# Graph attention on one core: seven block products inside one of the seven products of each 512x512 matrix product

## The chip, the cores and the metric

The kernel runs on one core of one Trainium2 chip. The metric is the device time of one execution in microseconds, and the number compared is the median over several executions. A second number, the span, comes from the profiler: the time from the first to the last instruction of one profiled execution.

The engines are named as in the profile: PE is the matrix engine (its weight loads are listed apart, as PEld), DVE the vector engine, ACT the scalar engine, POOL the general-purpose engine, and SP only starts transfers here.

## The reference

Two layers of graph attention on 128 graphs of 128 nodes with 512 features, all in fp32. `adj` is 128 matrices of 128x128.

```python
# layer 0 (8 heads of 64)
Q, K, V = x @ W_q + b_q, x @ W_k + b_k, x @ W_v + b_v
scores = einsum('bihd,bjhd->bhij', Q, K) / 8
scores = scores + (a[:, :, None] + c[:, None, :] + b_g + log(adj + 1e-9))   # a, c = x @ halves of w_g
x = einsum('bhij,bjhd->bihd', softmax(scores), V) + x
# layer 1
q, k, v = x @ Wq.T + bq, x @ Wk.T + bk, x @ Wv.T + bv
logits = einsum('bhqd,bhkd->bhqk', q, k) / 8 + log(clip(adj, 1e-8, None))
out = einsum('bhqk,bhkd->bhqd', softmax(logits), v) @ Wo.T + bo
return layer_norm(x + out) * gamma + beta
```

Of these only the seven 512x512 weight products per graph (three in layer 0, four in layer 1) are touched by the change.

## The kernel before

The graphs are worked on in groups of four, so there are 32 groups in each layer, and `t` counts the 64 of them. For every group each weight matrix is applied to 512 columns (four graphs of 128 nodes). This 512x512x512 product is cut in 2x2 blocks of 256 and done by Strassen's method in Winograd's form: seven products of 256x256x256 in place of eight, with sums of blocks ahead and behind. The sums of weight blocks are made once; the sums T1 to T4 of input blocks are made by POOL for each group.

```python
ORDER = ("P1", "P4 before", "P3 before", "P2", "P6", "P5", "P7")
OPERANDS = {
    "P1": (A11, "B11"), "P2": (A12, "B21"), "P3": (S4, "B22"), "P4": (NA22, "T4"),
    "P5": (S1, "T1"), "P6": (S2, "T2"), "P7": (S3, "T3"),
}
SUMS = {"T1": ("B12", "B11"), "T2": ("B22", "T1"), "T3": ("B22", "B12"), "T4": ("T2", "B21")}
```

`ORDER` is the order of a matrix's seven slots; "before" means the product belongs to the matrix before this one, so that two matrices overlap. One product is eight matmuls: two halves of the output, two of the depth, and each split in two column halves of 64 that write different halves of the partitions.

```python
def product(i, W, Bs, bank, side, first):
    a, b = Strassen.OPERANDS[i]
    a, b = W[:, a], Bs[b]
    for o in range(2):
        for k in range(2):
            ...                                  # dst: 256 columns of the bank, lhsT: 128x128, rhs: 128x256
            for half in HALVES:
                nc.tensor.matmul(dst[half], lhsT[:, half], rhs, start=(first and o == 0 and k == 0), stop=(k == 1),
                                 skip_group_check=True)
```

P1, P6, P7 and P4 add up in one bank of PSUM and are copied out by ACT between (t1, u2, u3); P5 and P3 share a second bank, P2 has a third. DVE adds.

```python
def unit(i):                                     # inside matrix()
    if i == "P1":
        t["W"], t["B"] = W(), Bs()
        t["a"] = bank(f"p{n % 2}")
    elif i == "P2":
        t["c"] = bank(f"p{(n + 1) % 2}")
    elif i == "P5":
        t["b"] = bank("p2")
    p = t[{"P2": "c", "P5": "b", "P3": "b"}.get(i, "a")]
    product(i, t["W"], t["B"], p, side, i in ("P1", "P2", "P5"))
    if i == "P1":   t["t1"] = kept("t1", p, 0)               # ACT copy, with the bias for q and k
    elif i == "P2": out_tile(); add(dst(0, 0), p, t["t1"])   # DVE
    elif i == "P6": t["u2"] = kept("u2", p, 0)
    elif i == "P7":
        t["u3"] = kept("u3", p, 1, 1)
        add(dst(1, 1), t["b"], t["u3"])                      # DVE
    elif i == "P4": copy(dst(1, 0), p, 1)                    # ACT
    elif i == "P3": add(dst(0, 1), p, t["u2"])               # DVE
```

Between the slots of the products lie a group's other steps, each put at a slot by number. `put(pre, i, ...)` sets a step ahead of slot i, `put(post, i, ...)` behind it; there are seven slots to a matrix, and every engine takes its instructions in this program order. In layer 0 the gate of each graph needs two sums of 512 products on DVE ("junk" in the profile), and POOL adds the bias row to the residual ("xn<-xn,bv", add_row).

```python
def gate(t, b, s):
    ...
    nc.vector.scalar_tensor_tensor(junk, XN[t, b // 2][:, b % 2], 1.0, WG[s], op0=ALU.mult, op1=ALU.mult,
                                   accum_out=C[t][:, s, b : b + 1])

def add_row(t, k):
    nc.gpsimd.tensor_tensor(XN[t, k], XN[t, k], wide(ROWS[split(t)[0]]), ALU.add)

def sums(Bs, name, tag, s):                      # T1 to T4, one buffer each
    a, b = Strassen.SUMS[s]
    Bs[s] = act.tile([P, 2, 2, N], F32, tag=f"{tag}{s}", name=f"{s}_{name}")
    nc.gpsimd.tensor_tensor(Bs[s], Bs[a], Bs[b], ALU.subtract)
...
if L == 0:
    for k, i in enumerate((6, 8, 9, 12, 14, 16, 18, 20)):
        put(post, first + i, gate, t, k // 2, k % 2)
    put(post, first + 20, gate_exp, t)
    for k in range(2):
        put(post, first + 21 + 2 * k, add_row, t, k)
```

`first` is the slot of v's P1 in group t. In layer 0 a group has the matrices v, q, k (slots 0 to 20); in layer 1 v, q, k and then o of the group before (28 slots). The scores of a group are made while the next two matrices run; its mixing with v follows three slots later.

Of the kernel before, what the change touches and what calls it, by code (L numbers as in the profile page):

```python
# [41 lines left out]
class Strassen:  # L42
# [6 lines left out]

    A11, A12, S4, NA22, S1, S2, S3 = range(7)  # L50

    ORDER = ("P1", "P4 before", "P3 before", "P2", "P6", "P5", "P7")
# [4 lines left out]
    SUMS = {"T1": ("B12", "B11"), "T2": ("B22", "T1"), "T3": ("B22", "B12"), "T4": ("T2", "B21")}  # L57

# [10 lines left out]
    @staticmethod  # L69
    def combine(v, t):  # L70
        v.tensor_tensor(t[:, Strassen.S1], t[:, Strassen.S3], t[:, Strassen.NA22], ALU.add)
        v.tensor_tensor(t[:, Strassen.S2], t[:, Strassen.S1], t[:, Strassen.A11], ALU.subtract)
        v.tensor_tensor(t[:, Strassen.S3], t[:, Strassen.A11], t[:, Strassen.S3], ALU.subtract)
        v.tensor_tensor(t[:, Strassen.S4], t[:, Strassen.A12], t[:, Strassen.S2], ALU.subtract)
        v.tensor_scalar_mul(t[:, Strassen.NA22], t[:, Strassen.NA22], -1.0)
# [26 lines left out]
def fast_path(ctx, tc, args, GOOD):  # L102
# [40 lines left out]
    def load_tiles(t):  # L143
        XT[t] = act.tile([P, G, KC, N], F32, tag="xT", name=f"xT_{t}", bufs=2)
        AD[t] = act.tile([P, G, N], F32, tag="adjT", name=f"adjT_{t}", bufs=3)
# [17 lines left out]
    def load(t):  # L163
        load_tiles(t)
        for b in range(G):
            load_graph(t, b, nc.sync)
        load_adjacency(t, nc.sync)
# [25 lines left out]
    def sums(Bs, name, tag, s):  # L193
        a, b = Strassen.SUMS[s]
        Bs[s] = act.tile([P, 2, 2, N], F32, tag=f"{tag}{s}", name=f"{s}_{name}")
        nc.gpsimd.tensor_tensor(Bs[s], Bs[a], Bs[b], ALU.subtract)


    def gate(t, b, s):

        if (b, s) == (0, 0):
            C[t] = small.tile([P, 2, G], F32, tag="c", name=f"c_{t}", bufs=3)
        junk = act.tile([P, D], F32, tag="oT3", name=f"junk_{t}_{b}_{s}")
        nc.vector.scalar_tensor_tensor(
            junk, XN[t, b // 2][:, b % 2], 1.0, WG[s], op0=ALU.mult, op1=ALU.mult,
            accum_out=C[t][:, s, b : b + 1],
        )
# [13 lines left out]

    def product(i, W, Bs, bank, side, first):
# [3 lines left out]
        a, b = W[:, a], Bs[b]  # L226
        for o in range(2):
            for k in range(2):
# [5 lines left out]
                for half in HALVES:  # L234
                    nc.tensor.matmul(
                        dst[half], lhsT[:, half], rhs, start=(first and o == 0 and k == 0), stop=(k == 1),
                        skip_group_check=True,
                    )

    def matrix(n, name, W, Bs, side, out_tile, dst, bias=None):  # L240


        t = {}

        def bank(tag):
            return ps.tile([P, 2, D2], F32, tag=tag, name=f"{tag}{name}")

        def shaped(v, o):
            return v.rearrange("p o (h d) -> p o h d", d=HD) if len(o.shape) == 4 else v

        def copy(o, i, m):

            if bias is None:
                nc.scalar.copy(o, shaped(i, o))
            else:
                for k in range(2):
                    c = 2 * m + k
                    nc.scalar.activation(o[:, k], i[:, k], AF.Identity, bias=bias()[:, c : c + 1])

        def kept(tag, i, m, bufs=2):  # L260
            o = work.tile([P, 2, D2], F32, tag=tag, name=f"{tag}{name}", bufs=bufs)
            copy(o, i, m)
            return o

        def add(o, i, v):
            nc.vector.tensor_tensor(o, shaped(i, o), shaped(v, o), ALU.add)

        def unit(i):
            if i == "P1":
                t["W"], t["B"] = W(), Bs()  # L270
                t["a"] = bank(f"p{n % 2}")
            elif i == "P2":
                t["c"] = bank(f"p{(n + 1) % 2}")
            elif i == "P5":
                t["b"] = bank("p2")
            p = t[{"P2": "c", "P5": "b", "P3": "b"}.get(i, "a")]
            product(i, t["W"], t["B"], p, side, i in ("P1", "P2", "P5"))
            if i == "P1":
                t["t1"] = kept("t1", p, 0)
            elif i == "P2":  # L280
                out_tile()
                add(dst(0, 0), p, t["t1"])
            elif i == "P6":
                t["u2"] = kept("u2", p, 0)
            elif i == "P7":
                t["u3"] = kept("u3", p, 1, 1)
                add(dst(1, 1), t["b"], t["u3"])
            elif i == "P4":
                copy(dst(1, 0), p, 1)
            elif i == "P3":  # L290
                add(dst(0, 1), p, t["u2"])

        return {i: (lambda i=i: unit(i)) for i in Strassen.OPERANDS}

    def v_matrix(n, t):
        L, _ = split(t)

        def tile_():
            V[t] = act.tile([P, G, H, HD + 1], F32, tag="v", name=f"v_{t}", bufs=2)
            nc.gpsimd.memset(V[t][:, :, :, HD : HD + 1], 1.0)  # L300
# [3 lines left out]
            lambda m, n: V[t][:, 2 * n : 2 * n + 2, 4 * m : 4 * m + 4, 0:HD],  # L304
        )

    def qk_matrix(n, t, which):
# [3 lines left out]
        def tile_():  # L311
            T[t] = act.tile([P, KC, G * N], F32, tag=f"{which}T", name=f"{which}T_{t}")
# [3 lines left out]
            lambda m, n: T[t][:, 2 * m : 2 * m + 2, n * D2 : (n + 1) * D2], lambda: bias[L],  # L316
        )

    def o_matrix(n, t):
        def tile_():  # L320
# [3 lines left out]
        return matrix(  # L324
            n, f"o_{t}", lambda: WO[1], lambda: TO[t], "x", tile_,
            lambda m, n: HS[t, n][:, :, m * D2 : (m + 1) * D2],
        )


    E = {}  # L330

    def scores(t, k):
# [4 lines left out]
        for b in (2 * k, 2 * k + 1):  # L337
            s[b] = ps.tile([P, 2, KC, N], F32, tag="s", name=f"s_{t}_{b}", bufs=2)
            rows = slice(b * N, (b + 1) * N)
            for c in range(KC):  # L340
                for r in range(2):
                    half = slice(r * HD, (r + 1) * HD)
                    nc.tensor.matmul(s[b][:, r, c], KT[t][half, c, rows], QT[t][half, c, rows], start=True, stop=True)
# [6 lines left out]
        for b in s:  # L350
            e = E[t, b]
            nc.vector.tensor_tensor(e, e, AD[t][:, b : b + 1].to_broadcast([P, H, N]), ALU.mult)

    def mix(t, graphs):
# [3 lines left out]
        for b in graphs:  # L358
# [3 lines left out]
            for h in range(H):  # L362
                for half in HALVES:
                    i = (h % KC) * (HD + 1)
                    nc.tensor.matmul(
                        a[b][half, h // KC, i : i + HD + 1], E[t, b][:, (h % 2) * KC + h // 2, half], V[t][:, b, h],
# [54 lines left out]
    def stats(t, b):  # L421
        if b == 0:
# [26 lines left out]
    def output_bias():  # L449

        p = ps.tile([P, 2, D2], F32, tag="p2", name="pbo")
        for m in range(2):
            for c in range(KC):
                nc.tensor.matmul(
                    p[:, m], bvcols[:, c], WO[1][:, Strassen.RAW[c // 2, m], c % 2],
# [6 lines left out]
    def strassen_weights(to, key, w, name, engine):  # L462
        to[key] = weights.tile([P, 7, 2, D2], F32, tag="w", name=name)
        Strassen.load(engine, to[key], w)
# [10 lines left out]
    def transposed(dst, src, name, copy, tag="t"):  # L475

        p = ps.tile([P, KC, N], F32, tag=tag, name=f"tr_{name}")
# [4 lines left out]
    for b in range(G):  # L482
        transposed(XT[0][:, b], XN[0, b // 2][:, b % 2], f"x_{b}", nc.vector.tensor_copy if b % 2 else nc.scalar.copy, ("t", "p2")[b % 2])
    TS[0] = quarters(XT[0])
    Strassen.combine(nc.vector, WV[0])
    for s in Strassen.SUMS:
        sums(TS[0], "0", "x", s)
    WG = [act.tile([P, D], F32, tag=f"oT{s + 1}", name=f"wg_{s}") for s in range(2)]
    for s in range(2):
        nc.sync.dma_start(WG[s], w_g[s * D : (s + 1) * D].partition_broadcast(P))  # L490
# [3 lines left out]
    ROWS[0] = row(nc, const, b_v0, "bv0")  # L494
# [3 lines left out]
    bvcols = act.tile([P, KC, P], F32, tag="oT4", name="bvcols")  # L498
    GA, BE = row(nc, const, gamma, "gamma"), row(nc, const, beta, "beta")
    ROWS[1] = row(nc, const, b_o1, "bo")  # L500
# [13 lines left out]
    for n in range(len(mats) + 1):  # L514
        for i in Strassen.ORDER:
            j, i = (n - 1, i[:2]) if "before" in i else (n, i)
            row_.append(mats[j][i] if 0 <= j < len(mats) else None)

    def slot(which, t, i):
        n = at[which, t] + ("before" in "".join(o for o in Strassen.ORDER if o.startswith(i)))  # L520
        return 7 * n + [o[:2] for o in Strassen.ORDER].index(i)

# [4 lines left out]

    for t in range(LAST):
        L, g = split(t)
        first = slot("v", t, "P1")  # L530

        a = slot("k", t, "P3") + 2
        put(pre, a, scores, t, 0)
        put(pre, a + 5, scores, t, 1)
        if t + 1 < LAST:
            put(pre, a + 3, mix, t, (0, 1))
            put(pre, a + 8, mix, t, (2, 3))
            put(post, a + 4, normalise, t, 0)
            put(post, a + 9, normalise, t, 1)
            put(post, a + 9, count, t)  # L540
        else:
            for b, i in enumerate((3, 4, 7, 8)):
                put(pre, a + i, mix, t, (b,))

        if t:
            put(post, first if L == 0 else first + 12, load_natural, t)
        if t + 1 < LAST:
            n = t + 1

            start = -1 if t == 0 else first + 7 if t > NG + 1 else first + 2  # L550
            put(post, start, load, n)
            start = max(start, 2)
            for b in range(G):
                put(post, start + 11 + b, lambda n, b: turn(XT[n][:, b]), n, b)
            put(post, start + 15, turn_adjacency, n)
            put(post, start + 15, lambda n: TS.update({n: quarters(XT[n])}), n)
            after = first + 20 if t <= NG else first + 25
# [336 lines left out]
```

## Time and profile before

| | |
|---|---|
| median of 3 executions | 3263.74 us (3263.38 to 3266.36) |
| span of the profiled execution | 3263.1 us |
| granted PE clock, mean | 0.998 |
| POOL, busy tenths in layer 0 and layer 1 | 2 to 3, and 5 |
| DVE, busy tenths in layer 0 and layer 1 | 5, and 4 |

The profile has a busy time for every engine, which says how full it is and not whether it is waited for. What sets the time is read from the chain of work that ended last (followed back from the last instruction) and from the list of waits, which names for each engine whom it waited for, with the total, the count and the longest. In the timeline a row is a run of equal instructions on one engine: its start, how long it lasted, what it writes and reads, and in brackets how long the engine had stood idle before and what ended that. The durations of rows of one engine overlap a little, since an instruction begins while the one before it drains.

The whole kernel is unrolled, and after the first group each layer repeats itself group by group. A group of layer 0 lasted 44.3 us (the T sums begin at 1017.76 and at 1062.03), one of layer 1 some 57 us.

### The profile page before, as it was taken

To read this page: it belongs to the slowest core of one execution; us is meant where nothing else is said; L and a number is where in the kernel's file an instruction comes from. 1 tells how busy PE (TensorE), PEld (TensorE's weight loads), DVE (VectorE), ACT (ScalarE), POOL (GpSimd) and SP (SyncE) were. 2 spreads that over 40 slices of the span, in tenths; PEclk is the share of its full clock that TensorE was granted. 3 is DMA by queue.
4 is the path that set the end of the run, shared out by engine and by line. 5 is a ranking of instruction groups with operands and counts; after the bars stand their busy time and mean duration, and the time that the engine had idled before them with its cause. 6 is when DMAs were issued, how large, how long until landed. Compare 5 with 4: busy or idle time off the path is not lost.

```text
span 3263.1 us, 87628 instructions
## 1 busy us (share of the span) xinstructions
PE 3235.5 (99%) x37346; PEld 2284.6 (70%) x37346; DVE 1649.2 (51%) x2817; ACT 1162.5 (36%) x2079; POOL 1525.2 (47%) x983
## 2 busy tenths in 40 slices
PE   9999999999999999999999999999999999999997
PEld 6777777777777777777676767777676767777674
DVE  5555555555555555554444444444444444444444
ACT  2333333333333333333333333333333333333332
POOL 2333323333333333463555555555555555555555
PEclk9999999999999999999999999999999999999999
DMA  5333333333333333342433334343434333343422
GB/s 127 85 79 79 78 83 66 85 85 75 77 81 73 78 86 78 89 104 52 91 73 76 88 73 93 69 99 65 96 68 78 86 74 91 70 98 66 101 63 72
DMA packets 1019062, 265.33 MB, mean 81 GB/s; under 512 B 944688, under 2 KB 951856, under 8 KB 1018672
## 3 DMA queue, kind: packets, MB, share of 16 engines
q1 hardware_dynamic: 1017584, 258.65, 35.3%
q8 instruction: 298, 4.88, 0.6%
q10 hardware_dynamic: 1088, 1.05, 0.1%
q14 instruction: 92, 0.75, 0.1%
HBM read 159.92 MB, written 67.11 MB: 70 GB/s over the span
## 4 chain that ended last, share of the span: by engine, by line
PE 99%; DMA 0%; POOL 0%; DVE 0%; ACT 0%; SPq 0%; issue 0%; ACTq 0%; DVEq 0%
PE p1v L99 11%; PE p0q L99 11%; PE p1k L99 11%; PE s L99 8%; PE av L99 7%; PE p2v L99 7%; PE p2q L99 7%; PE p2k L99 7%; PE p0o L99 7%; PE p1q L99 6%; PE p0k L99 6%; PE p0v L99 6%; PE p2o L99 3%; PE p1o L99 2%; PE po L99 0%; DMA wv<-in_L_gnn_W_v_dram 0%
## 5 line engine op out<-in xcount | busy, mean ns | idle before, releaser
L99 POOL TENSOR_TENSOR xn<-o,xn 128x1024 f32<-128x1024 f32 x64 | 149.0, 2328 | 749.6 <-DVE ok L99 454.3
L99 DVE TENSOR_TENSOR e<-e,adjT 128x1024 f32<-128x1024 f32 x256 | 321.8, 1298 | 241.8 <-ACT e L99 241.8
L99 POOL TENSOR_TENSOR xn<-xn,bo 128x1024 f32<-128x1024 f32 x64 | 158.5, 2496 | 344.3 <-DMA xn<-x1d 344.3
L99 PEld LDWEIGHTS av<-v,e 128*64 128x64 f32 x8192 | 261.0, 137 | 19.3 <-issue 0.9
L99 PEld LDWEIGHTS s<-qT,kT 64*128 64x128 f32 x4096 | 238.6, 188 | 49.2 <-issue 49.2
L99 PE MATMUL p1v<-wv,T 128*64 128x256 f32 x2256 | 268.3, 380 | 0.0
L99 PE MATMUL p0q<-T,wq 128*64 128x256 f32 x2256 | 267.5, 379 | 0.0
L99 PE MATMUL p1k<-T,wk 128*64 128x256 f32 x2256 | 267.5, 379 | 0.0
L99 POOL TENSOR_TENSOR T<-xT 128x512 f32<-128x512 f32 x128 | 183.0, 1430 | 177.8 <-DMA xn<-in_x_dram 127.8
L99 PE MATMUL s<-qT,kT 64*128 64x128 f32 x4096 | 263.1, 278 | 0.0
L99 PE MATMUL av<-v,e 128*64 128x65 f32 x8192 | 261.0, 221 | 0.0
L99 DVE SCALAR_TENSOR_TENSOR junk<-xn,wg 128x512 f32<-128x512 f32 x256 | 230.3, 900 | 0.0
L99 DVE STREAM_TRANSPOSE xT<-xT 128x512 f32<-128x512 f32 x252 | 173.4, 699 | 95.6 <-DMA xT<-x1d 95.2
L99 PEld LDWEIGHTS p0q<-T,wq 128*64 128x64 f32 x2256 | 163.0, 137 | 80.5
L99 PEld LDWEIGHTS p1k<-T,wk 128*64 128x64 f32 x2256 | 163.0, 137 | 80.5
L99 PEld LDWEIGHTS p1v<-wv,T 128*64 128x64 f32 x2256 | 161.1, 137 | 80.4
L99 DVE TENSOR_TENSOR qT<-p2q,u3q 128x512 f32<-128x512 f32 x64 | 44.3, 692 | 340.6 <-ACT u3q L99 340.6
L99 POOL TENSOR_TENSOR h<-h,xn 128x1024 f32<-128x1024 f32 x62 | 147.1, 2373 | 97.5 <-DVE h L99 86.5
L99 ACT ACTIVATE e<-s,c 128x1024 f32<-128x1024 f32 x128 | 135.8, 1112 | 134.8 <-PE s L99 134.8
L99 ACT COPY o<-av 128x520 f32<-128x520 f32 x256 | 151.7, 593 | 79.4 <-PE av L99 73.2
L99 PE MATMUL p0o<-wo,T_o 128*64 128x256 f32 x1488 | 178.0, 381 | 0.0
L99 ACT ACTIVATE e<-s 128x1024 f32<-128x1024 f32 x128 | 124.3, 1023 | 133.2 <-PE s L99 133.2
(159 smaller groups left out, 5972.4 us busy)
## 6 DMA issues: line engine op xcount, KB each, us to landing
xn<-in_x_dram SPq DMA_DIRECT2D x64, 512.0 KB, 4.2
x1d<-xn SPq DMA_DIRECT2D x64, 512.0 KB, 3.0
xT<-x1d SPq DMA_DIRECT2D x512, 64.0 KB, 2.4
xn<-x1d SPq DMA_DIRECT2D x64, 512.0 KB, 6.2
xT<-in_x_dram SPq DMA_DIRECT2D x496, 64.0 KB, 2.6
aT<-o SPq DMA_DIRECT2D x992, 32.0 KB, 2.0
out_dram<-h SPq DMA_DIRECT2D x62, 512.0 KB, 4.1
adjT<-in_adj_dram SPq DMA_DIRECT2D x256, 64.0 KB, 2.4
```

The lines of the kernel that those rows point to most:

```text
L99: return lambda *args, **kw: self.tc.keep_in_program_order(f(*args, **kw))
```

## The change

P2 (the product of A12 and B21, 256x256x256) is done by the same method once more: both operands are cut in blocks of 128, and seven products of 128x128x128 take the place of eight. Its purpose is to take an eighth of the multiplications of P2 away from PE. The inner sums of weights are made once, those of the input (`inner_sums`) by POOL for each group. The seven inner products share one bank (p1) with the output blocks as columns of it, in four phases, and between the phases DVE adds what has been summed so far onto t1. The first group (`inside=t > 0`) and the first o matrix keep the plain P2. In PSUM the bank of the former spare tag becomes a fourth bank for matrices: P1's bank alternates between p0 and p3, p2 is as before.

The order of everything else is set anew: the gate sums, the turns (transposes) of inputs, the POOL sums, the loads. The T sums get two buffers each, the adjacency two instead of three. The bias of q and k in block (0, 1) moves from ACT's copy u2 to DVE's addition for P3. The v and q/k tiles are laid out by blocks.

The diff, cut to what is spoken of (cuts marked by "..."):

```diff
-    ORDER = ("P1", "P4 before", "P3 before", "P2", "P6", "P5", "P7")
+    SLOTS = ("P1", "P2.1"), ("P4 b",), ("P3 b", "P2.2"), ("P6", "P2.3"), ("P5",), ("P7", "P2.4"), ()
+    PHASES = {"1": ("P1", "P2", "P5"), "2": ("P6",), "3": ("P7",), "4": ("P4", "P3")}
...
-        AD[t] = act.tile([P, G, N], F32, tag="adjT", name=f"adjT_{t}", bufs=3)
+        AD[t] = act.tile([P, G, N], F32, tag="adjT", name=f"adjT_{t}", bufs=2)
...
-        Bs[s] = act.tile([P, 2, 2, N], F32, tag=f"{tag}{s}", name=f"{s}_{name}")
+        Bs[s] = act.tile([P, 2, 2, N], F32, tag=s, name=f"{s}_{name}", bufs=2)
+    def inner_sums(Bs, name):
+        q = Bs["B21"]
+        y = act.tile([P, 4, N], F32, tag="inner", name=f"inner_{name}", bufs=2)
+        b11, b12, b21, b22 = q[:, 0, 0], q[:, 1, 0], q[:, 0, 1], q[:, 1, 1]
+        t1, t2, t3, t4 = (y[:, i] for i in range(4))
+        nc.gpsimd.tensor_tensor(t1, b12, b11, ALU.subtract)
+        nc.gpsimd.tensor_tensor(t2, b22, t1, ALU.subtract)
+        nc.gpsimd.tensor_tensor(t3, b22, b12, ALU.subtract)
+        nc.gpsimd.tensor_tensor(t4, t2, b21, ALU.subtract)
...
+        def onto(v, b, i, at):
+            v = v[:, b * N : (b + 1) * N]
+            nc.vector.tensor_tensor(v, i[:, at * N : (at + 1) * N], v, ALU.add)
+        def inner(phase):
+            v = t["t1"]
+            if phase == "1":
+                out_tile()
+                t["c"] = bank("p1")
+            p, a, b = t["c"], Strassen.inner_weight(*t["W"]), t["B"]["inner"]
+            for k, j in enumerate(Strassen.PHASES[phase]):
+                at = {"P2": 0, "P5": C12, "P3": C12}.get(j, C21)
+                x, y = (a[j], b[j]) if side == "w" else (b[j], a[j])
+                matmul(p[:, at * N : (at + 1) * N], x, y, phase == "1" and k == 0, True)
+            if phase == "1":
+                onto(v, 0, p, C21)
+                add(0, 0, p, v, 0, 1)
+            elif phase == "2":
+                onto(v, C12, p, C21)
+            elif phase == "3":
+                onto(v, 3, p, C21)
+                add(0, 0, p, v, 3, 4, C12 - 3)
+            else:
+                add(0, 0, p, v, 1, 3)
...
-                t["a"] = bank(f"p{n % 2}")
-            elif i == "P2":
-                t["c"] = bank(f"p{(n + 1) % 2}")
+                t["a"] = bank("p3" if n % 2 else "p0")
...
+                        for h, b in biased(0):
+                            nc.vector.scalar_tensor_tensor(o[:, h], p[:, h], b, t["u2"][:, h], op0=ALU.add, op1=ALU.add)
...
+        a = slot("k", t, 7)
+        for k in range(2):
+            put(pre, a + (4, 11 if t + 1 < LAST else 9)[k], scores, t, k)
+            for b in (2 * k, 2 * k + 1):
+                put(pre, a + (4, 11 if t + 1 < LAST else 9)[k], weigh, t, b)
+            if t + 1 < LAST:
+                put(pre, a + 7 + 7 * k, mix, t, (2 * k, 2 * k + 1))
...
+        n, late = t + 1, int(t > NG)
+                put(post, first + ((9, 13, 16, 17), (16, 17, 23, 24))[late][b], lambda n, b: turn(XT[n][:, b]), n, b)
+            put(post, first + (18, 26)[late], turn_adjacency, n)
+            put(post, first + (13, 17)[late], lambda n: inner_sums(TS[n], n), n)
+            for s in Strassen.SUMS:
+                put(post, first + (18, 24)[late], lambda n, s: sums(TS[n], n, s), n, s)
         if L == 0:
-            for k, i in enumerate((6, 8, 9, 12, 14, 16, 18, 20)):
+            for k, i in enumerate((0, 0, 2, 6, 13, 17, 18, 19)):
                 put(post, first + i, gate, t, k // 2, k % 2)
             put(post, first + 20, gate_exp, t)
             for k in range(2):
-                put(post, first + 21 + 2 * k, add_row, t, k)
+                put(post, first + 21 + k, add_row, t, k)
```

So in the program order of DVE around a boundary of two groups in layer 0 there now stand, one after another: k's phase 3 adds, a turn, a gate sum, the adjacency's turn and its scale, a gate sum, k's P7 add and phase 4 add, the last gate sum of the group; then v's phase 1 adds, two gate sums of the next group, k's P3 adds and v's phase 2 add. POOL has, from that same turn on: T1, T2, T3, T4, a memset of v's ones, add_row twice.

## The prediction

> **What bounds the kernel now.** I read the page's busy times first, then its chain, then who TensorE waited for, then the chain and the timeline inside one group of four graphs. From the page:
>
> ```profile
> PE 3235.5 (99%) x37346; PEld 2284.6 (70%) x37346; DVE 1649.2 (51%) x2817; ACT 1162.5 (36%) x2079; POOL 1525.2 (47%) x983
> ...
> PE 99%; DMA 0%; POOL 0%; DVE 0%; ACT 0%; SPq 0%; issue 0%; ACTq 0%; DVEq 0%
> ```
>
> TensorE (PE) is busy for the whole span, and the chain that ended last is PE for 99%. A busy PE need not be an efficient one, so the list of what PE waited for comes next:
>
> ```profile
> PE po L99 <- ACT aT_last L99: 6.8, 3, 5.3
> ...
> PE p1q L99 <- DVE v L99: 1.8, 1, 1.8
> ```
>
> These are waits at the end and the start; all its waits together are some 22 us, and none lies in the steady part. So time can be won only by giving PE less to do, and any wait that the change brings is added in full. What PE's work costs is read from the chain in a stretch of layer 0:
>
> ```profile
> 1028.29 1.88 PE p1v L99 x16
> 1030.17 1.73 PE p2v L99 x16
> 1031.89 1.73 PE p1v L99 x16
> 1033.62 1.87 PE av L99 x64
> ```
>
> One product (8 matmuls in the code, 16 records) takes 1.727 us: 1014.22 to 1015.94 and so on, always 1.72 or 1.73. The matmuls run as two half-columns side by side, so 8 steps of 215.9 ns. The mixing of two graphs (65 columns) has 32 such steps in 1.87 us, 58.4 ns each.
>
> **What the skill says.** The Trainium skill, "TensorE: Matmul & The Clock Gate", section "Back-to-back issue gap", gives N/2.4 + 2.5 ns between warm matmuls. With N = 512 this is 215.8 ns, which the trace meets if a 256-column fp32 record streams its columns twice; with 130 it is 56.7, and the trace has 58.4. So weight loads hide even behind 65 columns, and steps are paid by column. "SBUF — State Buffer", section "SBUF: two separate sides", says that VectorE (DVE) and GpSimd (POOL) share one port pair, held exclusively for a whole instruction, by any GpSimd operation and by a DVE operation with two SBUF inputs or in a two-port mode. This trace agrees, and the prediction rests on it:
>
> ```profile
> 1062.03 0.69 DVE L99 SCALAR_TENSOR_TENSOR junk<-xn,wg 128x512 f32<-128x512 f32 x1
> 1062.03 1.81 POOL L99 TENSOR_TENSOR T<-xT 128x512 f32<-128x512 f32 x1 [4.55 <-PE p2k L99]
> 1063.92 1.27 POOL L99 TENSOR_TENSOR T<-xT,T 128x512 f32<-128x512 f32 x1
> 1064.58 0.69 DVE L99 TENSOR_TENSOR kT<-p2k,u3k 128x512 f32<-128x512 f32 x1 [1.86 <-ACT u3k L99]
> 1065.16 1.27 POOL L99 TENSOR_TENSOR T<-xT 128x512 f32<-128x512 f32 x1
> 1065.19 1.78 DVE L99 SCALAR_TENSOR_TENSOR junk<-xn,wg 128x512 f32<-128x512 f32 x1
> 1066.39 2.81 POOL L99 TENSOR_TENSOR xn<-xn,bv 128x1024 f32<-128x1024 f32 x1
> ```
>
> The gate's sum (junk) takes 0.69 us alone, but 1.78 when POOL began 0.03 us before it: it ends 0.54 after POOL's end. POOL pays likewise (1.81 against 1.27). The addition that reads PSUM (kT) starts inside a POOL operation and still takes 0.69. At the start of the run a plain fp32 scale is held too:
>
> ```profile
> 15.41 1.72 POOL L99 TENSOR_TENSOR T<-T,xT 128x512 f32<-128x512 f32 x1
> 15.92 1.62 DVE L99 TENSOR_SCALAR wv<-wv 128x512 f32<-128x512 f32 x1
> ```
>
> (0.42 alone, at 19.99.) There four DVE and four POOL operations alternate: whoever waits gets the port when it is released, even if the other has its next operation ready.
>
> **What the change takes away.** P2 was 8 steps of 215.9 ns = 1.727 us. It becomes 7 block products, each two steps of 128 columns; the formula that fitted at 512 and 130 gives 256/2.4 + 2.5 = 109.2 ns a step, so 14 x 109.2 = 1.529 us. That saves 0.198 us in each matrix with the split: v, q, k in 63 groups (not the first) and o in 30, that is 219. 219 x 0.198 = 43 us, 1.3%. More cannot come: 3220 us is the floor.
>
> **What it adds, off the path.** Per matrix DVE gets five adds of 128 columns and one of 256 for one of 512. From rows of 692 ns (512) and 1230 (1024) an add costs 0.15 us + 1.05 ns a column: 0.285 and 0.42. That is some 1.2 us more, 250 us in all, on an engine with 1600 us free. POOL gets four 128-column sums a group, about 0.46 us each (1.28 at 512, 2.36 at 1024), twice that in most of layer 1: some 170 us of 1740 free. Neither becomes the bound by its total.
>
> **What it adds on the path.** Now PE waits for DVE between the phases, since they share a bank. Phases 1 to 2 are two products apart (3.45 us), 2 to 3 one product (1.73), 3 to 4 two (3.45), 4 to the next matrix's phase 1 one product (1.73, plus 1.87 where a mixing lies between). I lay DVE's and POOL's program order along PE's beat, with durations from the trace and time 0 at the end of k's P1 in layer 0.
>
> PE: phase 1 to 0.66, P4 2.38, P3 4.11, phase 2 4.33, P6 6.05, phase 3 6.27, P5 8.00, P7 9.73, phase 4 10.16, v's P1 11.89. There v's phase 1 needs DVE's last add on k's bank. ScalarE's copy of P7 ends 1.06 after P7 (it starts 0.22 late and takes 0.84), at 10.79; the 512-add and the 256-add then end at 12.53 - 0.68 = 11.85 if DVE is free. But before these DVE has, after phase 3's two adds (to 7.1), a turn (to 7.73), a gate sum, the adjacency's turn and scale, and another gate sum; and the same turn releases POOL's four T sums at 7.89, because T is now double-buffered. The gate takes the port at 7.66; T1 runs 8.20 to 9.47; the scale, 9.47 to 9.8; T2 was waiting, 9.8 to 11.0; the second gate, 11.0 to 11.56. The adds run 11.50 to 12.53. PE resumes at about 12.64, 0.11 after (at the start of the run it resumed 0.06 after DVE's end and lost 0.05 more for weights). **Wait one: 0.75 us.**
>
> DVE goes on with the last gate, which waits for T3 (to 12.83) and ends at 13.37; T4 runs to 14.64, and after a memset POOL starts add_row on 1024 columns at 14.67. The exponential of the gate (0.29) and v's t1 copy (0.59) follow the gate, so phase 1's two adds end at about 14.9 and the first of two gate sums of the next group asks for the port at 14.85: 0.18 us too late. It waits for add_row to 17.03; the second add_row, waiting, gets 17.57 to 19.93; the second gate ends at 20.47. Only then come k's P3 adds (two of 256) and v's phase 2 add, to 21.4; PE wanted phase 3 at 12.64 + 6.05 = 18.69 and gets 21.53. **Wait two: 2.84 us.** Then slack returns: POOL is idle in v's scores and q, and DVE is ahead at the next k.
>
> Together 3.6 us for each of 31 boundaries, +111 us. In layer 1 no gate sums exist. The score weighings (1.18 us) do meet POOL's T sums, but need to be ready only 3.9 us after the scores, and come out just in time. There q to k and k to o have no mixing between, and the add ends at 2.12 + 0.11 against PE's 2.16: 0.07 us in 62 places, +4 us. Sum: 3263.7 - 43 + 111 + 4 = 3335 us.
>
> **Rivals.** (1) Whoever wrote the new order knew the port, and its waits vanish: without the port my timetable has slack everywhere (0.35 us at wait one, 0.6 at wait two), and the result is 3263.7 - 43 + 4 = 3225. For it: before has no wait in its steady part though its gates do lose the port. Against it: before left 1.9 us behind such a gate; the new order leaves less than a POOL operation. (2) Half of it: wait two rests on 0.18 us; if the gate gets the port first, only one add_row stands in its way, and wait two is 0.7 us: 31 x 1.45 = 45, giving 3269. (3) The short steps are slower than the formula, because weights of 64 columns don't load in time: 58.4 ns at 65 columns speaks against it; 5 ns a step would cost 15 us. (4) Transfers: the adjacency has two buffers instead of three and is loaded later, but lands in 2.4 us, asked for some 14 us ahead; no change.
>
> **Range and chances.** I give the whole timetable about one half, the half-way case a fifth, and no port waits three tenths. The middle of that lies below 3335: I predict 3310 us. The low end is the floor with nothing going wrong, 3222; the high end the timetable plus some 20 us for short steps, 3355. Faster by over 2% (below 3198) is beyond what the change removes: 0.02. Slower by over 2% is above 3329, near the full timetable: 0.34. Within: 0.64.
>
> **What would show it.** A block step of 128 columns at 109 ns (P2 at 1.53 us over its phases) shows the saving right. In layer 0, PE should wait on DVE at v's phases 1 and 3, once a group, by 0.75 and 2.8 us, with gate sums of 2 to 3 us just ahead and POOL's T and add_row inside them. A layer 1 group should take about 0.8 us less than before. It is wrong if layer 0's groups also get shorter: then the port's order differs from what I took, most likely at 14.67 against 14.85.

## The result, and the profile after

The changed kernel takes 3260.19 us (median of 4 executions, 3258.34 to 3261.27), the kernel before, run beside it, 3264.43 us. The ratio is 0.9986, with a 95% interval of 0.9968 to 1.0003: of the 43 us that the block products take from PE, some 4 us arrive, and the interval (10 us shorter to 1 us longer) does not exclude that none does. The prediction was 3310 us.

The busy times and the chain that ended last, from the page of the changed kernel:

```profile
PE 3212.7 (99%) x39974; PEld 2358.3 (72%) x39974; DVE 2023.1 (62%) x4070; ACT 1133.6 (35%) x1951; POOL 1806.0 (55%) x1518
...
PE 90%; DVE 5%; SPq 2%; issue 2%; DMA 1%; ACT 0%; POOL 0%; DVEq 0%; ACTq 0%
```

PE is 23 us less busy than before, yet the span is only 4 us shorter (3259.4 against 3263.1), and the chain, which was PE for 99%, now runs through DVE for 5%. So PE has begun to wait for DVE. The list of what PE waited for (total us, times, longest) names where (p1v is the bank of v's block products, kT the tile that k's adds write):

```profile
PE p1v L124 <- DVE kT L124: 13.4, 31, 0.8
...
PE p1o L124 <- DVE kT L124: 3.4, 1, 3.4
...
PE p1q L124 <- DVE t1q L124: 1.0, 1, 1.0
```

The first comes once in every group of layer 0: v's phase 1 waits for k's last addition, as predicted ("wait one"). The list does not have the second predicted wait, 2.84 us at v's phase 3. The other two stand alone, where layer 0 ends.

To see what each stretch lost I take a group's length as the distance from the first mixing ("av") of one group to that of the next.

| us | layer 0 group (31) | two groups at the layer change | layer 1 group (30) |
|---|---|---|---|
| before | 44.27 | 92.3 | 56.36 |
| before, less 0.198 for each split matrix | 43.68 | | 55.57 |
| after | 44.44 | 98.8 | 55.79 |

Layer 0 gives back all that it won and a little more, layer 1 gives back 0.22 us a group, and the layer change costs 6.5 us. One boundary of two groups in layer 0, from the timeline of the changed kernel (the gate sums, "junk" before, are now "gw"):

```profile
1020.75 1.76 DVE L124 SCALAR_TENSOR_TENSOR gw<-xn,gw 128x512 f32<-128x512 f32 x1
...
1022.55 0.30 ACT L124 ACTIVATE gate<-c,bg 128x4 f32<-128x4 f32 x1 [0.67 <-DVE gw L124]
1023.04 0.41 DVE L124 TENSOR_TENSOR kT<-p1k,t1k 128x256 f32<-128x256 f32 x1
...
1023.50 0.66 PE L124 MATMUL p1v<-wv,xT 128*64 128x128 f32 x8 [0.41 <-DVE kT L124]
1023.60 1.71 POOL L124 TENSOR_TENSOR T<-T,xT 128x512 f32<-128x512 f32 x1
...
1025.03 0.83 DVE L124 SCALAR_TENSOR_TENSOR gw<-xn,gw 128x512 f32<-128x512 f32 x1
...
1025.33 5.51 POOL L124 TENSOR_TENSOR xn<-xn,row 128x1024 f32<-128x1024 f32 x2
...
1025.90 2.72 DVE L124 SCALAR_TENSOR_TENSOR gw<-xn,gw 128x512 f32<-128x512 f32 x1
...
1028.56 0.87 DVE L124 SCALAR_TENSOR_TENSOR kT<-p2k,bk,u2k 128x256 f32<-128x256 f32 x2
1029.35 0.28 DVE L124 TENSOR_TENSOR t1v<-p1v,t1v 128x128 f32<-128x128 f32 x1
...
1029.68 0.44 PE L124 MATMUL p1v<-wv,inner 128*64 128x128 f32 x4
```

The seventh gate sum, held by POOL, takes 1.76 us; behind it k's add is late, and PE resumes at 1023.50. (v's P1 began at 1021.20 and lasts 1.73, so PE wanted 1022.93: 0.57 us lost, and 0.05 more because the first record takes 0.66 and not 0.61. The list shows 0.41, since it counts from the modelled end of the last record.) At 1025.03 the first gate sum of the next group asks for the port while T4 still runs, and takes 0.83: it came ahead of the bias row. Only one addition of the bias row then stands before the second gate sum (2.72), and phase 3 starts at 1029.68 against a wanted 1029.61 (P6 began at 1027.88 and lasts 1.73).

### The profile page after: what moved, and what is told of

It reads as the page before. It is cut to its first block, busy times and chain, and to the rows that moved or that the text cites. A ratio compares the mean times of both kernels' runs of the same rounds, so it can differ in the third digit from the quotient of the medians.

```text
span 3259.4 us, 95184 instructions
## 1 busy us (share of the span) xinstructions
PE 3212.7 (99%) x39974; PEld 2358.3 (72%) x39974; DVE 2023.1 (62%) x4070; ACT 1133.6 (35%) x1951; POOL 1806.0 (55%) x1518
## 4 chain that ended last, share of the span: by engine, by line
PE 90%; DVE 5%; SPq 2%; issue 2%; DMA 1%; ACT 0%; POOL 0%; DVEq 0%; ACTq 0%
PE p0q L124 10%; PE p3v L124 9%; PE p3k L124 9%; PE s L124 8%; PE av L124 7%; PE p2v L124 7%; PE p2q L124 7%; PE p0o L124 6%; PE p2k L124 5%; PE p3q L124 3%; PE p2o L124 3%; PE p1v L124 3%; PE p1q L124 3%; PE p0k L124 3%; PE p1k L124 3%; DVE gw L124 2%
## 5 line engine op out<-in xcount | busy, mean ns | idle before, releaser
L124 POOL TENSOR_TENSOR xn<-xn,row 128x1024 f32<-128x1024 f32 x128 | 331.8, 2603 | 13.0 <-DMA xn<-x1d 10.0
L124 DVE SCALAR_TENSOR_TENSOR gw<-xn,gw 128x512 f32<-128x512 f32 x256 | 317.0, 1238 | 1.2
L124 PE MATMUL p3k<-T,wk 128*64 128x256 f32 x2256 | 268.5, 380 | 0.0
L124 PE MATMUL p3v<-wv,T 128*64 128x256 f32 x2256 | 267.4, 379 | 0.0
L124 POOL TENSOR_TENSOR T<-xT 128x512 f32<-128x512 f32 x128 | 219.3, 1713 | 84.5 <-DVE xT L124 83.9
L124 POOL TENSOR_TENSOR inner<-xT 128x128 f32<-128x128 f32 x126 | 67.5, 536 | 355.6 <-DMA adjT<-in_adj_dram 241.7
L124 POOL TENSOR_TENSOR h<-h,gamma 128x1024 f32<-128x1024 f32 x61 | 145.0, 2376 | 128.3 <-ACT h L124 128.2
L124 PEld LDWEIGHTS p3k<-T,wk 128*64 128x64 f32 x2256 | 159.5, 138 | 68.8 <-issue 1.3
L124 PEld LDWEIGHTS p3v<-wv,T 128*64 128x64 f32 x2256 | 159.0, 137 | 67.7
L124 DVE TENSOR_TENSOR t1q<-p1q,t1q 128x128 f32<-128x128 f32 x189 | 54.5, 288 | 188.5 <-PE p1q L124 187.4
```

The source lines that it names most:

```text
L124: return lambda *args, **kw: self.tc.keep_in_program_order(f(*args, **kw))
```

## The experiments

All edits are to the changed kernel; before ran at 3265.2 to 3265.5 us beside them.

**Making wait two happen.** The exponential of the gate reads only the first half of the sums, C[:, 0], which the seventh sum completes. Swapping the last two sums makes it wait for the eighth:

```diff
-                put(post, first + i, gate, t, k // 2, k % 2)
+                put(post, first + i, gate, t, k // 2, k % 2 if k < 6 else 7 - k)
```

> Edit: the last two gate sums of a layer 0 group change places, so that the exponential of the gate (and v's t1 copy behind it on ScalarE) needs the last one. Port theory (DVE and POOL alternate on the shared port): t1 copy comes some 0.9 us later, the first gate sum of the next group asks for the port after POOL's add_row has it, both add_rows run ahead of the two gate sums, and v's phase 3 waits some 2.7 us a group: 31 x 2.65 = 82 us more, about 3342 us. Rival (waits come from latency and a full DVE, not from the port): the 0.9 us fall into the 1.7 us that DVE has before k's P3, and the time stays at 3260.

Measured: 3365.09 us, ratio 1.031 (1.0292 to 1.0327). The list of PE's waits and the timeline of this kernel:

```profile
PE p1v L124 <- DVE t1v L124: 70.9, 31, 2.4
PE p1v L124 <- DVE kT L124: 13.4, 31, 0.8
```

```profile
1048.77 0.30 ACT L124 ACTIVATE gate<-c,bg 128x4 f32<-128x4 f32 x1 [2.35 <-DVE gw L124]
...
1049.88 5.11 POOL L124 TENSOR_TENSOR xn<-xn,row 128x1024 f32<-128x1024 f32 x2
...
1050.10 2.68 DVE L124 SCALAR_TENSOR_TENSOR gw<-xn,gw 128x512 f32<-128x512 f32 x1
...
1052.83 2.72 DVE L124 SCALAR_TENSOR_TENSOR gw<-xn,gw 128x512 f32<-128x512 f32 x1
...
1056.59 0.44 PE L124 MATMUL p1v<-wv,inner 128*64 128x128 f32 x4 [2.28 <-DVE t1v L124]
1056.96 3.68 PE L124 MATMUL s<-qT,kT 64*128 64x128 f32 x32
```

This is the predicted wait two: the gate sum asks 0.22 us after the bias row has taken the port, both sums lose it, and phase 3 waits 2.28 us. The order of two sums on one engine, with the same work, is worth 105 us. That is 23 us more than expected, and the last row says why: the scores take 3.68 us in place of 2.06. They did so after 18 of the 31 waits, 26 us in all, and groups last 48.4 us with it and 46.8 without. The last section says which waits these are. The table by stretches (length; busy time of PE, its weight loads, DVE, ACT, POOL; granted PE clock; DMA share; GB/s) shows half the clock during those scores and all of it afterwards:

```profile
1056.96:1058.80 1.84, 1.84 (x20) 1.84 (x20) 0.70 (x4) 0.07 (x1) 0.00 (x0) 0.53 0.64 102
1058.80:1060.60 1.80, 1.80 (x20) 1.62 (x18) 0.43 (x1) 1.11 (x1) 0.00 (x0) 0.54 0.56 89
1060.60:1064.00 3.40, 3.40 (x34) 2.32 (x34) 2.02 (x2) 1.11 (x1) 0.00 (x0) 1.00 0.62 98
```

**The same with the port free.** The kernel just shown, without the two additions of the bias row in layer 0 (its output lacks that row):

```diff
-            for k in range(2):
-                put(post, first + 21 + k, add_row, t, k)
```

> The slow kernel with the last two gate sums swapped (3365 us), with GpSimd's two additions of the bias row left out in layer 0 (its output lacks that row). Theory (the long wait of v's phase 3 needs two things, a late exponential of the gate and the bias row taking the shared port before the two gate sums): without the additions the gate sums take 0.7 to 0.8 us each in place of 2.7, v's phase 3 no longer waits, v's phase 1 still waits some 0.6 us for k, layer 0 groups about 44.4 us or less, about 3260 us. Rival (the late exponential by itself delays v's t1 copy and with it the phase 2 add, port or no port): the 2.4 us wait stays, layer 0 groups 46 us or more, 3320 to 3365 us.

Measured: 3256.05 us, ratio 0.9969 (0.9958 to 0.9979); layer 0 groups 44.30 us. From its timeline:

```profile
1022.04 0.68 DVE L124 SCALAR_TENSOR_TENSOR gw<-xn,gw 128x512 f32<-128x512 f32 x1
...
1022.76 0.69 DVE L124 SCALAR_TENSOR_TENSOR gw<-xn,gw 128x512 f32<-128x512 f32 x1
...
1026.09 0.39 PE L124 MATMUL p1v<-wv,inner 128*64 128x128 f32 x4
```

With the late exponential kept and the bias row gone, the sums take 0.68 us and phase 3 starts without a wait. The two sums stand in DVE's queue as before, and only POOL's additions are gone: it is the port that held them. Wait two needs both, the late exponential and the row. Wait one remains by itself: 44.30 - 43.68 = 0.62 us.

**What the new order costs without the blocks.** Every P2 is one plain product again. The block sums are still made, in place, so this product reads weight quarters that they have overwritten; its amount of work is that of the plain product:

```diff
-            if "." in i and inside:
+            if False:
```

> Edit: the new order kept, but every P2 done plainly as one product of 256 (no phases; the inner sums are still made). Theory (the split saves 0.198 us a matrix on PE, and the phases' waits give back 0.75 us a group in layer 0 and 0.22 in layer 1): PE gets 43 us more work and loses the waits, groups last 44.27 and 56.36 us as in the kernel before, total about 3267. Rival (the new order by itself costs PE time, the split has no waits): the time is 3260 + 43 = 3303.

Measured: 3269.61 us, ratio 1.0013 (1.0006 to 1.0020); layer 0 groups 44.27, layer 1 groups 56.36 in nearly half of the cases and 56.5 to 56.9 in the others. PE waits for no block add. The order by itself costs 4 us, and in the profiled executions they lie in layer 1, whose 30 groups take 1694.8 us against 1690.7 before.

**k's 256-column add first.** Phase 1 of the next matrix needs only the add on phase 4's bank; the add of P7, which stood ahead of it, is put behind:

```diff
             elif i == "P7":
                 kept("u3", p, 1, 1)
-                add(1, 1, t["b"], t["u3"])
...
-                return inner(i[-1])
+                inner(i[-1])
+                if i == "P2.4":
+                    add(1, 1, t["b"], t["u3"])
+                return
```

> Edit: DVE's phase 4 add stands ahead of P7's add, so that p1 is free without waiting for ScalarE's u3. Theory (layer 1: latency of copy and two adds; layer 0: the chain of alternating DVE and POOL operations on the port sets when k's P3 adds and v's phase 2 add are done): layer 1 loses its 0.22 us a group (55.57), layer 0 keeps 44.4 because the wait moves from v's phase 1 to v's phase 3; total 3253. Rival (each wait stands alone): layer 0 also loses 0.6 us a group, 43.8, total 3235.

Measured: 3253.95 us, ratio 0.9965 (0.9952 to 0.9977). Of 30 layer 1 groups 17 take 55.57 us, so the 0.22 us are gone there; the others are longer for another reason (below, "Not foreseen"). Layer 0 stays at 44.44, because the wait moved, as its list of waits says:

```profile
PE p1v L124 <- DVE t1v L124: 15.6, 30, 0.5
```

Phase 1 now starts in time, so phase 3 wants its operand 0.5 us earlier, and the 2.72 us gate sum holds it up.

**Clearing the port.** Three of the six gate sums and one of the two additions of the bias row leave the stretch between k's phase 3 and v's phase 3:

```diff
-            for k, i in enumerate((0, 0, 2, 6, 13, 17, 18, 19)):
+            for k, i in enumerate((0, 2, 6, 6, 6, 13, 13, 19)):
...
-                put(post, first + 21 + k, add_row, t, k)
+                put(post, first + (9, 22)[k], add_row, t, k)
```

> Edit: three gate sums moved away from the boundary of groups (slots 0,2,6,6,6,13,13,19) and the first add_row moved to slot 9, where POOL is idle; nothing else. Port theory: v's wait at phase 1 falls from 0.62 to about 0.1 us (copy and adds alone), phase 3 waits for nothing, layer 0 groups last 43.8 us, total 3240. Rival (DVE's amount of work or the latency of the phases sets the wait): the amount of work is the same, groups stay at 44.4, total 3260.

Measured: 3239.31 us, ratio 0.9920 (0.9903 to 0.9937); layer 0 groups 43.79 us, layer 1 unchanged at 55.79. For wait one the edit clears DVE's queue and the port together. With the queue alone DVE would not have been late: from 1018.75 on, two gate sums, a turn and a scale at their undisturbed 0.68, 0.68, 0.70 and 0.43 us end by 1021.3, ahead of the copy u3 that the adds need (1021.88, at the end of ACT's row `u3k`, which began at 1021.04). In the changed kernel they ended at 1022.5.

**Both of these edits.**

> The changed kernel with both edits at once: VectorE's last two adds of P7 moved behind phase 4's add, and the gate sums and the bias row moved out of the stretch between two matrices. Theory (the 0.22 us per layer 1 group and the layer 0 waits are the adds that stand in the vector queue ahead of the next matrix's first block product, and, in layer 0, the port that holds them up; once the port is clear, the order of the adds decides): layer 0 groups 43.7 us, layer 1 groups 55.57 us, 3239.3 - 31 x 0.1 - 31 x 0.22 = about 3229 us. Rival (what is left after the port is cleared is the cost of the extra block instructions on TensorE itself, so the order of the adds gives nothing more): layer 0 stays at 43.8 us, layer 1 at 55.8 us, the time at 3239 us.

Measured: 3233.60 us (3225.98 to 3234.84), ratio 0.9896 (0.9879 to 0.9912). Layer 0 groups are 43.67 us and half of the layer 1 groups 55.57, which is the kernel before less 0.198 for each matrix: once the port is clear, the order of the adds gives its part in both layers. The median lies 4 us above the 3229 expected (one of the four executions took 3226); the other layer 1 groups last up to 56.7.

**The layer change.** In the changed kernel the first output projection waits 3.4 us. Its timeline:

```profile
1518.47 1.30 DVE L124 STREAM_TRANSPOSE aT<-aT 128x512 f32<-128x512 f32 x2 [4.01 <-DMA adjT<-in_adj_dram]
1519.70 0.65 DVE L124 TENSOR_TENSOR kT<-p2k,u3k 128x512 f32<-128x512 f32 x1
...
1520.74 2.58 PE L124 MATMUL p1o<-wo,aT 128*64 128x256 f32 x16 [3.38 <-DVE kT L124]
...
1523.10 3.00 PE L124 MATMUL p3k<-T,wk 128*64 128x256 f32 x16
```

DVE idles for 4 us on two transposes that wait for a transfer, and k's adds stand behind them. The two products after the wait take 2.58 and 3.00 us in place of 1.9: from 1521.91 to 1525.32 the granted clock was 0.50. So the wait cost some 1.8 us above its own length. The edit, on top of both others, puts the second pair of transposes (and POOL's sums of the same input) one place later for this group:

```diff
-                turned = f + 18
+                turned = f + 18 + (t == NG)
```

> The kernel with both edits, and at the layer change alone the two transposes of aT that VectorE makes after a transfer put one place later, behind k's last adds. Theory (the single 3.4 us wait of the first output projection is k's last adds standing in the vector queue behind transposes that wait for a transfer): that wait goes, 3.4 to 4 us less than the kernel with both edits alone, about 3226 us. Rival (the output projection needs those transposes soon after anyway, so the wait only moves): within 1 us of the kernel with both edits.

Measured: 3226.81 us (3225.56 to 3228.52), ratio 0.9885 (0.9868 to 0.9901). The wait is gone, and the two groups at the layer change take 93.1 us in place of 97.6, so 4.5 us are the edit's. The rest of the difference of 6.8 us is not: between the two profiled executions it lies in layer 1, where fewer groups are long, and in the last groups. Beside the row of the changed kernel, the gate sums show the cleared port:

```profile
L124 DVE SCALAR_TENSOR_TENSOR gw<-xn,gw 128x512 f32<-128x512 f32 x256 | 317.0, 1238 | 1.2
```

```profile
L124 DVE SCALAR_TENSOR_TENSOR gw<-xn,gw 128x512 f32<-128x512 f32 x256 | 190.5, 744 | 3.6 <-DMA gw<-in_L_gnn_w_g_dram 0.2
```

The first is the changed kernel's (mean 1238 ns), the second that of the kernel with the three edits (744).

**The three edits with the plain P2.** The last kernel with the edit `if False:` of above, to see whether the edits win anything without the blocks.

> The kernel with the three mends (adds of P7 last, port cleared between matrices, turn of aT after k's adds), but with every P2 one plain product again in place of the block products. It still makes the block sums, which overwrite quarters of the weights that the plain product then reads, so its output lacks the right values. Theory (the mends win nothing by themselves, they only let the blocks' saving through): layer 0 groups 44.27 us, layer 1 groups 56.36 us as in the kernel before, some 3264 to 3267 us, so that the blocks are worth 38 to 41 us under the mended order. Rival (the mended order is faster in itself, whatever P2 is): below 3255 us, and the blocks are worth less than 30 us.

Measured: 3269.78 us, ratio 1.0014 (1.0007 to 1.0021), layer 0 groups 44.27. The edits win nothing there. Under the same order the block products are worth 3269.8 - 3226.8 = 43.0 us.

## Why the prediction was wrong

**The saving: right.** 219 x 0.198 = 43 us was predicted, 43.0 is measured between the last two kernels. A block step takes 109 ns as worked out: ahead of the boundary shown above, phase 4's two block products begin at 1020.76 and 1020.98 and the next P1 at 1021.20, so each has its two steps in 0.22 us. The section cited for the formula gives it for an isolated matmul, and for a stream in which each matmul has its weight load about 81 ns at N=128 and 131 at N=512. Here every matmul had its load, and 215.9 and 109 ns were measured: the measurement decides, and the forecast took the right one of the page's figures.

**The chain ahead of phase 1: right, a little too long.** It was to be gate, T1, scale, T2, gate and then k's adds, and the trace has that order. Wait one was given as 0.75 us and is 0.62.

**Wait two: the step that failed.** The prediction said: "The exponential of the gate (0.29) and v's t1 copy (0.59) follow the gate, so phase 1's two adds end at about 14.9 and the first of two gate sums of the next group asks for the port at 14.85: 0.18 us too late." The exponential does not follow the last gate sum. It reads the half that the seventh sum completes, and ran at 1022.55, before the eighth had begun. Counted as in the prediction (time 0 at 1011.04, the end of k's P1), the first gate sum of the next group asks at 13.99, not 14.85, and T4 still runs. So it gets the port ahead of the bias row, and one addition of the row, not two, stands before k's P3 adds. Where I had 2.84 us, some 0.14 are left (44.44 against the 44.30 without the bias row; in the boundary shown 0.07, and 0.05 because the record takes 0.44 and not 0.39). The rest of that mechanism was sound: with the exponential made to wait for the eighth sum, the gate sum comes 0.22 us late, both sums lose the port and phase 3 waits 2.3 us. Everything hung on 0.18 us, as the text said. The fault was to take the dependence from the word "gate" and not from the column that is read. The sign of being wrong that I had named, shorter layer 0 groups, did not appear (44.44 against 44.27); the missing wait at phase 3 did.

**The sum.** 31 x 3.6 = 111 us was given for layer 0; it is 31 x (44.44 - 43.68) = 23.6 us. Of the 87 us between, 84 are wait two (31 x 2.70). My rival "half of it" foresaw the true order of the port and had a fifth of the weight; its 3269 came within 9 us in part by luck, since it gave wait two 0.7 us where 0.14 are left, 17 us too much in all, and had no losses at the layer change. Half of the weight lay on the full timetable, which drew 3310 some 50 us too high. The range of 3222 to 3355 held the result by its width.

**Layer 1.** A group took 56.36 us before, not some 57. I gave 0.07 us for each of q to k and k to o, and 0.8 us less for a group, where my own terms make 4 x 0.198 - 2 x 0.07 = 0.65. Measured: 0.11 each, so 0.22 a group, and 0.57 less. At one change from q to k:

```profile
2403.48 0.84 ACT L124 ACTIVATE u3q<-p0q,bq 128x256 f32<-128x256 f32 x2 [3.10 <-PE p0q L124]
2403.64 1.90 PE L124 MATMUL p3k<-xT,wk 128*64 128x256 f32 x16
...
2404.96 0.41 DVE L124 TENSOR_TENSOR qT<-p1q,t1q 128x256 f32<-128x256 f32 x1
...
2405.43 0.66 PE L124 MATMUL p1k<-xT,wk 128*64 128x128 f32 x8
```

P7 ended at 2403.20. The term that was mis-sized is the copy of P7: it ends 1.12 us after P7 and not 1.06, so the last add ends at 2.17 and not at 2.12. The resumption was as given: 0.06 us after the add, and 0.05 more because the record takes 0.66 and not 0.61.

**Not foreseen.** Between the two profiled executions the span is 3.7 us shorter where 43.4 were to be won, so 39.7 us did not arrive. With the saving counted in each stretch, 24.2 of them lie in layer 0 (its 31 groups take 1378.2 us, 1372.4 before), 9.7 in layer 1 (30 groups, 1676.6 and 1690.7) and 7.5 at the layer change; start and end together are 1.6 us better. The layer change I did not foresee; between the last two edited kernels 4.5 us went with the later transposes. Nor did I foresee that layer 1 loses more than its 30 x 0.22 = 6.6 us: four groups are longer than the others, the longest by 1.7 us:

```profile
2086.36 0.29 DVE L124 TENSOR_TENSOR h<-p1o,t1o 128x128 f32<-128x128 f32 x1 [4.08 <-DMA out_dram<-h]
...
2086.79 0.44 PE L124 MATMUL p1o<-woi,inner_o 128*64 128x128 f32 x4 [1.48 <-DVE h L124]
```

There DVE's add onto h waits for a store of h to the output, and o's phase 2 waits for that add. The same wait accounts for about half of what the longer layer 1 groups cost the kernels with the add moved (7 such waits in the first of them, up to 0.5 us; 8 with the port cleared too, up to 0.9). Why the store is late there is not shown, and no run moves it. DVE and POOL grew by 374 and 281 us, not by 250 and 170; they did not become the bound, and part of the growth is the time for which the port holds them (the gate sums alone are 127 us longer than with the cleared port).

## What to carry to other kernels

A saving on an engine that is busy all the time comes through only if nothing late stands ahead of its operand in another engine's queue: here the same blocks were worth 4 us or 39 us, by where some gate sums, a row addition, one add and two transposes were put. When a forecast rests on who takes a shared port first, find for each link the one element it reads, since a dependence on the seventh sum rather than the eighth was worth 105 us (some 29 of them by the halved clock, 18 groups of 1.6 us). And move a mend's whole chain: the earlier add alone did nothing in layer 0, because the next wait on the same port took its place.

## What the runs showed of the hardware

**A wait can cost more than its length, by where it falls.** After PE had stood idle for 2.28 us until 1056.59, its granted clock was 0.50 from 1057.06 to 1060.47; so it went in 18 of 31 cases. After the 3.4 us at the layer change it fell to 0.50 too, 1.2 us into the work that followed. After waits of 0.4 to 0.5 us it never did: all whole rows of scores there take 2.06 us. In the clock record of the kernel with the late exponential each of the 18 half-speed stretches lasts 3.41 us, and their starts lie whole multiples of 3.413 us apart (28 for the first two, at 101.33 and 196.90). This fixed grid tells the waits apart: where 2.11 to 2.30 us of idle time fell into one window of it, the next window had half the clock; the 13 waits that it cut in two, with at most 2.02 us in one window, were spared. The layer change of the changed kernel fits: 2.24 of its 3.38 us lie in the window that ends at 1521.91. The Trainium skill, "TensorE: Matmul & The Clock Gate", section "What's actually happening", says that the clock is halved after an idle window of about 3.4 us, that the window runs freely, and that about as long a busy window restores it. The length, the free run and the time to restore agree with this trace; but the window did not have to be idle throughout, since 2.11 us of it sufficed, and there the measurement decides.

**The port is handed over, and small operations are held too.** The gate sum of 1025.90 (2.72 us, 0.69 with the port free) ended at 1028.62, between the ends of two additions of the bias row (1028.08 and 1030.84) that POOL had ready one behind the other. At the layer change, while POOL made the weight sums, an operation of 16 columns ("gated") took 1.13 us at 1441.19; with POOL idle, at 1458.27, 0.17.
